# Four GpSimd operations of a recurrent layer moved to marked places in the step, and the product r put ahead of v

## The chip, the cores and the metric

The kernel runs on one core of one Trainium2 chip. The metric is the device time of one launch in microseconds: 3721.07 us, the median of 3 runs (3719.92 to 3722.31). Everything is float32.

A core has a TensorE for matrix products (PE in the profile; PEld are its weight loads), VectorE (DVE), ScalarE (ACT) and GpSimd (POOL) for elementwise work, and SyncE (SP), which issues most transfers. Each takes its own instructions in the order of the program and waits for the others by semaphores. GpSimd also issues some DMAs here, those that add into memory.

## What is computed

Four blocks follow each other on a tensor x of 4 batches x 512 tokens x 512 channels: a cross attention (layer 0), two recurrent layers of the RWKV kind (layers 1 and 2) and a resampler attention with an MLP (layer 3). The change touches only the recurrent layers. Both compute, for each batch, with `state` taken from the second input:

```python
xa = _ln(x, ln1_w, ln1_b)
sx = concatenate([state[:, 1][:, None], xa[:, :-1]], axis=1) - xa     # token differences
t = tanh((xa + sx * maa_x) @ maa_w1)                                  # then five mixes m
mw, mk, mv, mr, mg = ...                                              # t @ maa_w2, 5 x 512 channels
xw = xa + sx * (maa_w + mw)                                           # and xk, xv, xr, xg alike
w = exp(-exp(time_decay + tanh(xw @ decay_w1) @ decay_w2))
r, k, v = xr @ Wr.T, xk @ Wk.T, xv @ Wv.T
g = silu(xg @ Wg.T)
def step(s, (k, v, w, r)):                                            # per head, 16 x 16 state
    a = k[:, None] * v[None, :]
    return a + w[:, None] * s, einsum('s,st->t', r, u * a + s)
y = normalised(outs) * gn_w + gn_b                                    # per head
x = x + y * g @ Wo.T                                                  # time mixing
x = x + sigmoid(xr2 @ fWr.T) * (relu(xk2 @ fWk.T)**2 @ fWv.T)         # channel mixing, own norm and shift
```

The term `r * u * a` of the output needs no recurrence: it is v times the sum over a head's channels of r u k. The kernel calls that sum `al`.

## The kernel before

`recurrent` (from L455) works in 16 **units**: 2 layers x 4 batches x 2 halves of 256 tokens. A unit has 8 **steps**, one for each of 8 groups of state rows (two halves `e` of the value channels times four `i`). The main loop (L1078 and after) runs over a global step number g; step 0 to 7 of a unit in the text is g modulo 8. Two tokens are folded into one place of a scan, so that the scan has half as many places: the kernel keeps the tokens of a unit as firsts and seconds, and corrects for the fold with small products (`rk`, `D`, and the changed second half of r and first half of k).

One turn g of the loop issues, in this order:

- `summed(g - 1)` (L878): TensorE sums ry over state rows into PSUM tile py.
- `begun(g + 1)` (L825): VectorE makes kv and A, each a product of vr (v repeated over partitions, in PSUM) with o_k (L833), and copies the state into kv's column 0 (L839). GpSimd issues a DMA that adds A onto kv (`added`, L584). ScalarE copies the decays into W (L844). There are two kv buffers and one A.
- `scan(g)` (L860): VectorE's scan over kv with W (L866), then two products ry of kv with o_r (L871).
- every second half unit `repeated` (L808): TensorE makes vr from o_v.
- then what is due at this place of the step's four **phases** EARLY, SOON, MID, LATE. `mixes`, `outputs` and `channels` are generators; each `yield s, phase` says when its next part is issued, in steps from its unit's step 0. `mixes(q)` runs ahead of its unit (negative numbers), `outputs` and `channels` behind it. So in one turn of the loop three units are at work: with unit u in step 6, `mixes` prepares units u + 1 and u + 2, `outputs` finishes u - 1, `channels` u - 2.

The parts of `mixes(q)` that matter, with their places before: layer norm statistics (`stats`) at -11 LATE, `scaled` (z, ScalarE) at -10 EARLY, `turned` (transposes ptn on TensorE, emptied by ScalarE into xa) at -9 EARLY, `shift` (token differences sx, GpSimd, L588 and L589) at -9 MID, mixx at -9 LATE; the products k at -5 MID, v at -4 MID, r at -3 MID (for unit 0: r, then v), g at -2 MID, its gate (o_g, VectorE, L717) at -2 LATE. A product ends in ScalarE copies out of PSUM (L702); r's also makes `ruk`, r times u (L705). GpSimd multiplies ruk by k at -2 EARLY (L772). At step 0 TensorE forms al (L73), and at 0 LATE GpSimd makes y from v and al (L799) and adds rk to its second half (L800).

`outputs` normalises y: mean, squares, var, two powers on GpSimd (L933, L935), rp (ScalarE, L939), pbc (TensorE) and bc (ScalarE) at 13 EARLY, y times bc at 13 LATE (L946), then yg: scaled on ScalarE (L951), times g on GpSimd (L958), at 14 EARLY, and the product with Wo at 15 MID, added to x by VectorE (L973). `channels` has its own statistics, scaling, transposes (xc), shift (sxc) and products fk, fr, fv.

TensorE's products all use the line of the helper `mm` (L73), except those with 32 columns (L689 for v and g, L814 vr, L885 py). They share three PSUM buffers. Weights are loaded ahead into four SBUF buffers from SyncE's queue, in the order in which the products stand.

## Time and profile before

| What | us |
|---|---|
| median of 3 runs | 3721.07 (3719.92 to 3722.31) |
| span of the profiled execution, first to last instruction | 3715.9 |
| first scan to last scan of the recurrent layers, from the span's start | 780.6 to 2241.9 |
| busy in the span: TensorE, VectorE, ScalarE, GpSimd | 3545.8, 2728.7, 1675.7, 1743.4 |

The profiled execution's own time is its span; what lies outside the span (the launch's beginning and end) is in the runs' times only. A row of the timeline view reads: start, duration, engine, line, operation, what it writes <- what it reads, sizes (out<-in), how many equal ones are merged, and in brackets how long the engine was idle before it and what ended that. A row of the groups view reads: line, engine, operation, names, sizes, count | busy us, mean ns of one | idle us before them and what ended it. A row of stretches gives from:to and length, then the busy us of PE, PEld, DVE, ACT and POOL with their instructions, the granted share of TensorE's clock, the DMA engines' busy share and GB/s.

### The profile page before, as it was taken

How to read it: one execution, taken by the hardware profiler on the slowest of the kernel's cores; microseconds unless marked ns; L12 is line 12 of the kernel's file. 1: busy time of each engine (PE TensorE's matmuls, PEld its weight loads, DVE VectorE, ACT ScalarE, POOL GpSimd, SP SyncE). 2: the span in 40 equal slices, each digit the busy share in tenths (PEclk: the TensorE clock that was granted, in tenths of full speed). 3: DMA queues.
4: the chain of work that ended last, by engine and by line, in shares of the span. 5: the costliest groups of instructions: out<-in, count | busy, mean ns of one | idle time of the engine just before them, and what ended most of it. 6: DMA issues, size and time to landing. Idle time of an engine off the chain costs nothing. (4 is left out here: it accounts for less than half of the span.)

```text
span 3715.9 us, 52436 instructions
## 1 busy us (share of the span) xinstructions
PE 3545.8 (95%) x20544; PEld 1885.9 (51%) x20544; DVE 2728.7 (73%) x4601; ACT 1675.7 (45%) x2550; POOL 1743.4 (47%) x850
## 2 busy tenths in 40 slices
PE   8999999998899999999999988999999999999989
PEld 3333333365566665666666644444455444544446
DVE  6777777679988888888888883388855676667531
ACT  4777676544444444444444433233344334434421
POOL 4777777524444444444444443065533343444430
PEclk9999999999999999999999998999999999999999
DMA  4000000056677777777777775300022212121223
GB/s 154 24 12 24 12 9 21 24 130 140 146 177 175 177 187 182 176 175 177 177 175 177 177 167 134 102 26 18 23 88 77 72 52 88 60 71 35 97 97 125
DMA packets 188806, 386.67 MB, mean 104 GB/s; under 512 B 18128, under 2 KB 44880, under 8 KB 186512
## 3 DMA queue, kind: packets, MB, share of 16 engines
q1 hardware_dynamic: 150256, 251.72, 21.2%
q0 software_dynamic: 38304, 131.61, 19.4%
q8 instruction: 162, 2.65, 0.3%
q14 instruction: 84, 0.69, 0.1%
HBM read 247.50 MB, written 4.19 MB: 68 GB/s over the span
## 5 line engine op out<-in xcount | busy, mean ns | idle before, releaser
L1253 POOL TENSOR_TENSOR acc<-acc,aT 128x2048 f32<-128x2048 f32 x96 | 436.2, 4544 | 336.2 <-ACT aT L1248 219.6
L292 POOL TENSOR_TENSOR aT<-aT,nmT 128x1536 f32<-128x1536 f32 x124 | 428.6, 3460 | 206.1 <-ACT aT L290 182.8
L254 DVE CUSTOM_DVE_ANT_0 sc<-psc,nm 128x512 f32<-128x512 f32 x512 | 353.8, 691 | 146.8 <-PE psc L242 89.1
L1237 DVE TENSOR_TENSOR aT<-pst,mb 128x512 f32<-128x512 f32 x512 | 317.5, 681 | 163.2 <-PE pst L1192 163.2
L871 DVE TENSOR_TENSOR ry<-kv,o_r 128x1024 f32<-128x1024 f32 x256 | 398.6, 1598 | 7.2 <-PE pm L73 0.5
L866 DVE TENSOR_TENSOR_SCAN kv<-W,kv 128x1032 f32<-128x1032 f32 x128 | 295.9, 2311 | 0.0
L584 POOL DMA_DIRECT2D kv<-A x127 | 111.4, 877 | 358.0 <-DVE kv L839 220.0
L290 ACT COPY aT<-pst 128x512 f32<-128x512 f32 x372 | 196.5, 594 | 177.2 <-PE pst L279 176.8
L298 ACT ACTIVATE aT<-aT 128x2048 f32<-128x2048 f32 x128 | 246.7, 1929 | 5.5 <-POOL aT L292 4.8
L73 PE MATMUL ph<-nT,l_m 128*128 128x256 f32 x1024 | 235.9, 385 | 0.0
L73 PE MATMUL po<-l_m,hT 128*128 128x512 f32 x512 | 233.1, 601 | 0.0
L73 PEld LDWEIGHTS ph<-nT,l_m 128*128 128x128 f32 x1024 | 191.8, 191 | 64.2 <-issue 24.8
L1206 DVE CUSTOM_DVE_ANT_0 sc<-psc,zeros,mx 128x512 f32<-128x512 f32 x256 | 176.6, 745 | 56.2 <-PE psc L1192 47.1
L279 PE MATMUL pst<-q,km 32*128 32x512 f32 x1024 | 206.3, 639 | 9.4 <-DVE mxs L254 5.8
L1248 ACT ACTIVATE aT<-aT 128x2048 f32<-128x2048 f32 x64 | 122.3, 1910 | 190.6 <-DVE aT L1237 185.7
L1246 ACT ACTIVATE aT<-aT,mc 128x2048 f32<-128x2048 f32 x64 | 128.1, 2002 | 162.6 <-DVE aT L1237 156.3
L1206 DVE CUSTOM_DVE_ANT_0 sc<-psc,nm 128x512 f32<-128x512 f32 x256 | 161.1, 684 | 52.2 <-PE psc L1192 52.2
L242 PE MATMUL psc<-km,q 32*128 32x512 f32 x1024 | 197.8, 650 | 0.8 <-ACT q L223 0.8
L885 PE MATMUL py<-ry,k 128*32 128x512 f32 x1024 | 161.9, 625 | 38.3 <-DVE ry L871 25.6
L1192 PE MATMUL pst<-q,kT 32*128 32x512 f32 x1024 | 183.1, 649 | 0.0
L1192 PE MATMUL psc<-kT,q 32*128 32x512 f32 x1024 | 171.0, 644 | 12.3 <-DVE aT L1237 11.5
L1251 POOL TENSOR_TENSOR acc<-aT 128x2048 f32<-128x2048 f32 x16 | 72.5, 4532 | 234.2 <-ACT aT L1246 234.2
(266 smaller groups left out, 6999.6 us busy)
## 6 DMA issues: line engine op xcount, KB each, us to landing
l_m<-in_L_W SPq DMA_DIRECT2D x64, 1024.0 KB, 5.1
kv<-A POOLq DMA_DIRECT2D x127, 516.0 KB, 6.1
L_wk<-in_L_Wk SPq DMA_DIRECT2D x16, 1024.0 KB, 8.0
L_wr<-in_L_Wr SPq DMA_DIRECT2D x16, 1024.0 KB, 7.2
L_wv<-in_L_Wv SPq DMA_DIRECT2D x16, 1024.0 KB, 5.8
L_wg<-in_L_Wg SPq DMA_DIRECT2D x16, 1024.0 KB, 7.6
L_wo<-in_L_Wo SPq DMA_DIRECT2D x64, 256.0 KB, 4.9
L_fk<-in_L_fWk SPq DMA_DIRECT2D x16, 1024.0 KB, 6.8
```

The lines of the kernel that those rows point to most:

```text
L73: nc.tensor.matmul(ps, lhsT, rhs, start=(i == 0), stop=(i == len(pairs) - 1))
L242: nc.tensor.matmul(psc, d["q"][g][rs, lt * P : (lt + 1) * P], d["km"][rs, a, :], start=True, stop=True, tile_position=(32 * r, 0),)
L254: nc.vector.tensor_tensor_reduce(sc, ps[r], d["nm"][lt], 1.0, -3.0e38, ALU.add, ALU.max, mxs[:, a, lt, c : c + 1])
L279: nc.tensor.matmul(pst, d["km"][rs, a, s * P : (s + 1) * P], d["q2", a][rs, :], start=True, stop=True, tile_position=(32 * r, 0),)
L292: nc.gpsimd.tensor_tensor(w[:, n:, :], w[:, n:, :], nmT[:, None, :].to_broadcast([P, NR - n, L]), ALU.add)
L298: nc.scalar.activation(w, w, AF.Exp)
L866: nc.vector.tensor_tensor_scan(flat(kv), flat(W[g % 2]), flat(kv), 0.0, ALU.mult, ALU.add)
L871: nc.vector.tensor_tensor(y, kv[:, 4 * h : 4 * h + 4, None, :TP].to_broadcast([P, 4, 2, TP]), d["r"][:, i].rearrange("p (o m) -> p o m", o ...
L1192: nc.tensor.matmul(psc, lhsT[rs], rhs[rs], start=True, stop=True, tile_position=(32 * r, 0))
L1206: nc.vector.tensor_tensor_reduce(sc, ps[r], d["nm"][a], 1.0, mx[:, 0, lt, r : r + 1] if a else 3.0e38, ALU.add, ALU.min, mx[:, a, lt, r : ...
L1237: nc.vector.tensor_tensor(w[:, r, :], ps[r], d["mb"][:, r, :], ALU.subtract)
L1253: nc.gpsimd.tensor_tensor(d["acc", m], d["acc", m], w, ALU.add)
```

## The change

Four operations on GpSimd are no longer issued where their generator stands, but put into a list for a global step (`pooled`, `slots`): sx at step -9, ruk times k at -2, y at 1, its second sum at 2. `begun(g + 1)`, in turn g, issues that turn's list: after VectorE's kv and A products it first lets GpSimd copy one element per partition of kv into a new tile `mark`, which waits for kv's product, then issues the list, and only then the DMA that adds A onto kv. For units 0 and 1 the operations at negative steps are issued at once. The state's copy into kv's column 0 stands ahead of the kv and A products instead of behind them. r is made ahead of v in every unit. Statistics, scaling and transposes of `mixes` stand one step earlier from unit 2 on.

In the order of the instructions, in a unit of the middle: on TensorE r, py, pbc, v, py, vr, 16 transposes (xc and xa), g, py, Wo (before: v, py, pbc, r, py, vr, 8 transposes, g, py, 8 transposes, Wo). On ScalarE rp follows r's copies and the ruk scalings, the two z of the token mixing stand ahead of bc, and xa's copies ahead of yg. On VectorE the statistics stand in step 4 ahead of mix_g, and mixx ahead of the two additions to x. On GpSimd: mark, ruk, kv<-A, yg, sxc, mark, sx, kv<-A, xk, xr. Nothing else is added or removed but the marks.

```diff
@@ recurrent
+        mark = lp.tile([P, 1], F32, name="mark")
...
         st = {}
+        slots = {}
+
+        def pooled(q, at, f, *args):
+
+            if q < 2 and at < 0:
+                f(*args)
+            else:
+                slots.setdefault(G * q + at, []).append(lambda: f(*args))
@@ mixes
-            yield -12 if q == 1 else -10, EARLY
+            yield -12 if q == 1 else -11, EARLY
             z = scaled("mix", tiles, nm, rstd)
-            yield -11 if q == 1 else -9, EARLY
+            yield -11 if q == 1 else -10, EARLY
             turned(z, vec, cur, V_LN1W, V_LN1B)
...
-            yield -11 if q == 1 else -9, MID
+            yield -11 if q == 1 else -10, MID
...
-            shift(sx, cur, stT[:, :, b, 1] if hf == 0 else st[q - 1]["last"])
+            pooled(q, -9, shift, sx, cur, stT[:, :, b, 1] if hf == 0 else st[q - 1]["last"])
...
             yield -4, MID
-            if q > 0:
-                product("v")
-            else:
-                ruk = mp.tile(full, F32, tag="mix", name="ruk", bufs=BUFS["mix"])
-                product("r")
+            ruk = mp.tile(full, F32, tag="mix", name="ruk", bufs=BUFS["mix"])
+            product("r")
+            k, r = d["k"], d["r"]
+            pooled(q, -2, nc.gpsimd.tensor_tensor, ruk, ruk, k, ALU.mult)
             yield -4, LATE
             mixed("g")
             yield -3, MID
-            if q > 0:
-                ruk = mp.tile(full, F32, tag="mix", name="ruk", bufs=BUFS["mix"])
-                product("r")
-            else:
-                product("v")
+            product("v")
+            if q == 0:
                 repeated(0, 0)
             yield -2, EARLY
-            k, r = d["k"], d["r"]
-            nc.gpsimd.tensor_tensor(ruk, ruk, k, ALU.mult)
...
-            nc.gpsimd.tensor_tensor(y, d["v"], al[:, None, :].to_broadcast(full), ALU.mult)
-            nc.gpsimd.tensor_tensor(seconds(y), seconds(y), rk, ALU.add)
+            pooled(q, 1, nc.gpsimd.tensor_tensor, y, d["v"], al[:, None, :].to_broadcast(full), ALU.mult)
+            pooled(q, 2, nc.gpsimd.tensor_tensor, seconds(y), seconds(y), rk, ALU.add)
@@ begun
+            nc.vector.tensor_copy(quarters(kv)[:, :, :, 0], states(q)[:, i, e])
             for half, dst in ((seconds, kv), (firsts, A)):
                 nc.vector.tensor_tensor(
...
-            nc.vector.tensor_copy(quarters(kv)[:, :, :, 0], states(q)[:, i, e])
+            large = slots.pop(g - 1, ())
+            if large:
+                nc.gpsimd.tensor_copy(mark, kv[:, 0, 1:2])
+            for f in large:
+                f()
@@ the loop's start
-                follow(q, (-13 if q == 1 else -11, LATE), mixes(q))
+                follow(q, (-13 if q == 1 else -12, LATE), mixes(q))
```

## The prediction

> **What bounds the kernel now.** I read the page's busy shares first, then the recurrent stage (780 to 2250 us, the only one the diff touches) by stretches, then one unit of it in order of time, engine by engine.

> ```profile
> PE 3545.8 (95%) x20544; PEld 1885.9 (51%) x20544; DVE 2728.7 (73%) x4601; ACT 1675.7 (45%) x2550; POOL 1743.4 (47%) x850
> ...
> L871 DVE TENSOR_TENSOR ry<-kv,o_r 128x1024 f32<-128x1024 f32 x256 | 398.6, 1598 | 7.2 <-PE pm L73 0.5
> ```

> TensorE is the wall on average, but ry takes 1598 ns in the mean where its shortest is 1209 (view of tile ry): something lengthens it. By stretches (PE, PEld, DVE, ACT, POOL busy):

> ```profile
> 780.00:1037.00 257.00, 218.53 (x1738) 142.03 (x1737) 242.64 (x234) 109.08 (x223) 107.48 (x72) 0.93 0.64 143
> 1037.00:2090.00 1053.00, 1011.19 (x6890) 642.21 (x6889) 915.18 (x937) 490.35 (x1008) 483.31 (x341) 1.00 0.77 178
> ```

> Units 0 to 2 are bound by VectorE (242.6 of 257 us), units 3 to 13 by TensorE; scans eight steps apart show a unit to last 95.4 us there. The end of one such unit, TensorE:

> ```profile
> 1576.52 0.70 PE L73 MATMUL pbc<-rp,gsel 128*128 128x256 f32 x2 [0.74 <-ACT rp L939]
> 1577.06 7.63 PE L73 MATMUL pm<-mix_r,L_wr 128*128 128x256 f32 x32
> ...
> 1586.68 1.09 PE L572 MATMUL ptn<-ident,z 128*128 128x128 f32 x8
> 1587.71 7.14 PE L689 MATMUL pm<-mix_g,L_wg 128*32 128x256 f32 x128
> 1594.66 1.04 PE L885 MATMUL py<-ry,k 128*32 128x512 f32 x8
> ...
> 1596.89 0.66 PE L572 MATMUL ptn<-ident,z 128*128 128x128 f32 x4 [0.59 <-DVE o_g L717]
> 1597.53 7.11 PE L73 MATMUL pm<-L_wo,yg 128*128 128x512 f32 x16
> 1605.43 2.19 PE L885 MATMUL py<-ry,k 128*32 128x512 f32 x8 [0.80 <-DVE ry L871]
> ```

> The last row matters: py waits 0.80 us for the first ry, and takes 2.19 instead of 1.04 because the second ry is late as well. So one chain per unit ends last: g product, its gate o_g (ScalarE, then VectorE), step 7's kv, A, scan and two ry, then py and al. VectorE and GpSimd there:

> ```profile
> 1597.35 1.22 DVE L833 TENSOR_TENSOR kv<-vr,o_k 128x1024 f32<-128x1024 f32 x1
> 1598.48 1.21 DVE L833 TENSOR_TENSOR A<-vr,o_k 128x1024 f32<-128x1024 f32 x1
> ...
> 1599.68 2.30 DVE L866 TENSOR_TENSOR_SCAN kv<-W,kv 128x1032 f32<-128x1032 f32 x1
> 1602.02 4.50 DVE L871 TENSOR_TENSOR ry<-kv,o_r 128x1024 f32<-128x1024 f32 x2
> ```

> ```profile
> 1595.44 1.89 POOL L588 TENSOR_TENSOR sxc<-xc 128x1020 f32<-128x1020 f32 x1
> ...
> 1602.07 2.22 POOL L588 TENSOR_TENSOR sx<-xa 128x1020 f32<-128x1020 f32 x1
> 1603.92 1.51 POOL L589 TENSOR_TENSOR sx<-stT,xa 128x4 f32<-128x4 f32 x1
> ```

> The two ry take 4.50 beside sx and 2.36 where GpSimd is quiet (at 1574.56): 2.14 us lost. ruk does the same in step 6 (4.54 at 1585.13), y in step 0 (4.32 at 1518.46). sxc, beside o_g and kv, which read PSUM, lengthens nothing. The question is what the marked place does to the **scan**, which reads W and kv, both in SBUF. One place answers:

> ```profile
> 2241.88 3.98 DVE L866 TENSOR_TENSOR_SCAN kv<-W,kv 128x1032 f32<-128x1032 f32 x1
> ```

> ```profile
> 2240.84 2.86 POOL L588 TENSOR_TENSOR sxc<-xc 128x1020 f32<-128x1020 f32 x1
> ```

> A scan that comes up while sxc runs takes 3.98 instead of 2.30 and ends 2.2 us after sxc does: it waited for it. (At 1517.08 y starts inside a scan and takes 3.49: there GpSimd waited.) So whoever comes second waits, scans included.

> **The change, part by part.** Zero is 1567.83, where TensorE starts the first of the two products v and r in that unit; g ends at 26.83 (1594.66).

> 1. *r ahead of v.* pbc waits for rp, which ScalarE copies behind the product's own eviction. Behind v that is one o_v copy, and pbc starts 1.78 after py (1574.74 to 1576.52). Behind r the row at 1584.72 (o_r, 0.59) is followed by the ruk scalings (to 1586.05) and only then by rp (1.00): 2.43 after py. **+0.65.** vr then follows v with one py between: o_v's last copy ends 0.84 after that py starts, vr is due 0.99 after: nothing. The weight loads of r and v only change places on SP's queue, one product (7 us) apart.

> 2. *Layer norm, scaling and transposes a step earlier.* TensorE now turns four tiles (xc, xa) ahead of g instead of two: 2 x 0.515 (1586.68 to 1587.71) = **+1.03**. There are three PSUM buffers; ScalarE starts emptying 0.70 after the first tile and takes 0.97 a tile, so tile 4 waits 0.18 and g 0.45: **+0.63.** g ends 0.65 + 1.03 + 0.63 = 2.31 later, at 29.14. The 0.59 wait of the second ptn behind o_g goes, but that was beside the chain, not in it.

> 3. *From g to step 7.* Now kv starts 2.69 after g's end (1594.66 to 1597.35), because the o_g row on ScalarE (1595.51) waits for yg on GpSimd to free the buffer. After, yg's scaling follows xa instead of z (2.07 instead of 1.43 behind xc), yg ends at about 28.9, just before g; o_g then costs its own copies and gate, 1.70. **-1.0.** Were yg 1 us later, this gain would be gone.

> 4. *sx at its mark in step 7.* kv 1.21, then the mark. No row has a 128x1 copy on GpSimd; the nearest small ones are 0.21 (L589 beside sxc) and 0.84 (L552, blocked), so with its wait 0.15 to 0.9, and I take 0.3, near the first. sx by start-to-start spacing is 1.85 (1602.07 to 1603.92). It ends 3.4 after kv's start; the scan, due at 2.3, waits 1.1. Then scan 2.30, 0.1 for L589, two ry 2.36, and 0.07 for the moved state copy: 8.2 instead of 9.17. **-0.95.** The mark delays what is queued behind it on GpSimd: kv<-A by some 3.5 us (its second half waits for the scan), xk and xr by some 2.5. kv<-A was issued at 1600.32, lands in 4.6 in this step, and the next A comes at 1610.35: 5.4 of slack. xk lands some 6 us ahead of its product. Both covers hold.

> Sum for units 3 to 13: 0.65 + 1.03 + 0.63 - 1.0 - 0.95 = +0.36, 11 units: **+4**. TensorE would be ready for py 1.8 us ahead of ry, so the chain decides. y (step 1), its sum (step 2) and ruk (step 6) save or cost VectorE 0.4 to 2 us each, but VectorE then waits anyway (4.07 for o_g, 3.70 for S, 1.33 for mean): nothing. kv<-A behind y keeps 2.7 to 3.5 us of slack in step 1, less the 2.1 that y adds.

> [...] GpSimd's rows overlap (sx 2.22 from 1602.07, L589 from 1603.92). [...] By the printed 2.22 the unit would come to 0.37 more, 4 us in all; the duration 1.89 of the undisturbed sxc speaks for the spacing.

> 5. *Units 0 to 2.* Where VectorE decides, each move gains ry's loss and pays the scan's: y 2.0 against 1.35, ruk 2.0 against 1.35, sx 1.5 against 1.15, and the sum in step 2 newly costs 0.45 of a scan. Against it, the layer norm's 1.9 us of VectorE now stands ahead of step 5's A, and the next A waits for the DMA of that one (1.67, 1.60, 1.71 us in these units), so it moves 1.9. In unit 0 the gate also comes later, with g behind the transposes: the A at 840.89 becomes about 842.5, and o_g 854 instead of 851.1. By unit +2.5, 0, +0.5: **+3**. Bounds -8 (every contention gone) and +8.

> 6. *Units 14 and 15.* rp's 0.65 once; in unit 15 ry gains 2, which A gives back waiting for its DMA (it waited 0.97 already), and the sum costs 0.45: **+1.**

> Total 4 + 3 + 1 = +8 to +9. The profiled span of 3715.9 us becomes about 3724.5; the median shown, 3721.07, lies 5.2 above the span, and I carry that: **3730 us.**

> **Rivals.**
> *A, the forecast (0.58).* The mark moves the collision from ry to the scan, and g comes later. Own range 3718 to 3744: per unit -0.3 to +1.2 (mark 0.15 to 0.9, yg in time or not).
> *B, faster (0.21).* GpSimd's operations fit beside A, and the scan doesn't wait. Step 7 then takes 7.0, TensorE decides, and al starts at 38.4 instead of 39.7: -1.3 x 11 = -14, and units 0 to 2 gain 8: 3700 us (3692 to 3712). For it: 51 of 52 scans beside GpSimd are not lengthened. Against it: in those GpSimd had come second. It decides if sx ends within about 2.3 us of kv's start.
> *C, nothing (0.12).* Each move trades like for like, TensorE's order absorbs the rest: 3721.
> *D, clearly slower (0.09).* GpSimd reaches the mark late. It must finish sxc 1.0 us ahead of kv's end; if ScalarE's longer way to yg eats that, sx falls behind the scan and ry pays 2.1 as before, while g is still 2.3 later: +1.3 to +2.3 a unit, +8 for the rest: 3746 (3739 to 3752).

> **How the numbers follow.** A measurement of this kernel tells about 0.2% (7.4 us) from no change. A's range lies above 3728.5 in two thirds of its cases and within in the rest: slower 0.39 + 0.09 = 0.48, same 0.19 + 0.12 = 0.31, faster 0.21. The range 3704 to 3748 leaves out half of B and of D, some 0.16.

> **What would show it.** Right: ry near 1230 ns throughout and scans in steps 1, 6 and 7 at 3.3 to 3.8; pbc waiting about 1.4; two ptn rows in front of g with a wait ahead of it; py in step 7 still waiting for ry, by more than 0.8. Wrong: scans at 2.30 with ry at 1.2 (B), or ry still at 3.3 in step 7 (D), or a unit shorter than 95 us.

## The result, and the profile after

The changed kernel takes 3775.61 us, the median of 4 runs (3774.95 to 3777.61), against 3720.57 (3719.92 to 3722.31) before: 1.0148 times as long, 95% interval 1.0133 to 1.0162. That is 55 us more, where the prediction had 9 and a range that ended at 3748.

The span of the profiled execution grew by 60.0 us, 3715.9 to 3775.9. Scans eight steps apart tell where:

| Stretch of the profiled span | before | after | more | forecast |
|---|---|---|---|---|
| start to first scan | 780.6 | 783.2 | 2.6 | 0 |
| units 0 to 2 | 256.9 | 269.4 | 12.4 (unit 0 alone: 10.3) | 3 |
| unit 3 | 97.1 | 97.8 | 0.8 | 0.4 |
| units 4 to 13 | 955.6 | 989.6 | 34.0 | 3.6 |
| start of unit 14 to last scan | 151.7 | 155.9 | 4.2 | 1 |
| behind the last scan | 1474.1 | 1480.0 | 6.0 | 0 |

The page of the changed kernel has these lines (engine and line, names, sizes, count, then busy us and mean ns, then idle us ahead of them and what ended it):

```profile
PE 3572.3 (95%) x20544; PEld 1898.9 (50%) x20544; DVE 2674.5 (71%) x4601; ACT 1676.0 (44%) x2550; POOL 1751.0 (46%) x910
...
L874 DVE TENSOR_TENSOR_SCAN kv<-W,kv 128x1032 f32<-128x1032 f32 x128 | 337.2, 2634 | 0.2 <-DMA kv<-A 0.2
L879 DVE TENSOR_TENSOR ry<-kv,o_r 128x1024 f32<-128x1024 f32 x256 | 303.8, 1228 | 6.8
...
L837 DVE TENSOR_TENSOR A<-vr,o_k 128x1024 f32<-128x1024 f32 x128 | 155.7, 1217 | 59.0 <-DMA kv<-A 58.9
```

VectorE is busy 54 us less: ry fell from 1598 to 1228 ns, and the scan rose from 2311 to 2634. So the collision did move from ry to the scan, and in VectorE's busy time the move paid. But A, a single buffer, waited 59 us in all for the transfer that adds it onto kv, against 17.5 before:

```profile
L833 DVE TENSOR_TENSOR A<-vr,o_k 128x1024 f32<-128x1024 f32 x128 | 155.3, 1213 | 17.5 <-DMA kv<-A 17.4
```

Half of the 59 fall into units 3 to 13, where none of TensorE's waits ends with them; of the rest, 8.35 us in unit 0 cost time, as a run below shows.

The stretches, units 0 to 2 and units 3 to 13 (columns as in the prediction):

```profile
783.00:1052.00 269.00, 227.12 (x1736) 145.46 (x1735) 229.03 (x234) 108.31 (x223) 106.13 (x83) 0.88 0.60 134
1052.00:2147.00 1095.00, 1028.93 (x6913) 650.13 (x6912) 884.13 (x944) 492.48 (x1011) 493.01 (x386) 0.99 0.74 173
```

VectorE, which bound units 0 to 2 with 242.6 of 257 us, now waits there: 229.0 of 269. TensorE in a unit of the middle; the places that the prediction spoke of:

```profile
1611.22 0.70 PE L73 MATMUL pbc<-rp,gsel 128*128 128x256 f32 x2 [1.29 <-ACT rp L947]
...
1622.61 0.66 PE L573 MATMUL ptn<-ident,z 128*128 128x128 f32 x4 [0.24 <-ACT xc L575]
1623.52 7.14 PE L698 MATMUL pm<-mix_g,L_wg 128*32 128x256 f32 x128 [0.25 <-ACT xc L575]
...
1639.04 2.19 PE L893 MATMUL py<-ry,k 128*32 128x512 f32 x8 [0.46 <-DVE ry L879]
1641.16 1.99 PE L73 MATMUL al<-ruk,ksel 128*128 128x256 f32 x8
...
1649.59 7.14 PE L73 MATMUL pm<-xk,L_fk 128*128 128x256 f32 x32 [1.97 <-issue]
```

Up to al all is nearly as forecast. Then the product fk waits 1.97 us, where in the kernel before it had waited for nothing:

```profile
1612.09 1.91 PE L633 MATMUL pm<-mixx,L_w 128*32 128x256 f32 x8
1613.94 7.17 PE L73 MATMUL pm<-xk,L_fk 128*128 128x256 f32 x32
```

The view names only "issue", but xk's transfer landed at 1649.50, 0.09 us ahead of this row, and that distance is 0.09 us in each of units 3 to 13. GpSimd there:

```profile
1633.54 0.19 POOL L845 COPY mark<-kv 128x1 f32<-128x1 f32 x1 [1.21 <-DVE kv L837]
1633.68 1.89 POOL L589 TENSOR_TENSOR sx<-xa 128x1020 f32<-128x1020 f32 x1
1635.53 2.21 POOL L590 TENSOR_TENSOR sx<-stT,xa 128x4 f32<-128x4 f32 x1
1637.67 0.88 POOL L585 DMA_DIRECT2D kv<-A  x1
1638.26 1.18 POOL L585 DMA_DIRECT2D xk<-xc  x1
```

ScalarE had xk ready at 1634.1; it waited behind the mark, sx, the small second part of sx (2.21 us: it came up during the scan, which ended at 1637.73, and ended at 1637.74) and kv<-A. And the transfer itself was slower. The view of tile xk, units 3 to 13, before and then after:

```profile
DMA to landing us min/median/max: 6.3/6.4/6.6
```

```profile
DMA to landing us min/median/max: 11.0/11.2/11.5
```

The weights L_wk, 1 MB from SyncE's queue, start when Wo ends (0.03 us behind it, before and after). Before, that was 3.15 us behind xk's issue; after, 0.4 us (xk's issue and L_wk's before, then L_wk's after, beside the xk row above):

```profile
1601.51 0.86 POOL L584 DMA_DIRECT2D xk<-xc  x1 [0.31 <-ACT xk L996]
1604.66 0.37 SPq L63 DMA_DIRECT2D L_wk<-in_L_Wk  x1
```

```profile
1638.62 0.37 SPq L63 DMA_DIRECT2D L_wk<-in_L_Wk  x1
```

L_wk became slower as well: in units 3 to 13 it lands 9.4 to 10.4 us after its issue, where it took 7.9 to 8.2.

A unit grows for one more reason, the granted clock (share of TensorE's clock is the third figure from the end):

```profile
1662.89:1666.30 3.41, 2.91 (x17) 1.92 (x18) 3.00 (x3) 2.65 (x7) 0.01 (x1) 1.00 0.47 165
1666.30:1669.71 3.41, 3.41 (x5) 1.35 (x4) 3.41 (x5) 0.85 (x3) 3.14 (x5) 0.50 0.64 121
1669.71:1673.13 3.42, 3.42 (x9) 1.52 (x8) 3.39 (x3) 0.08 (x1) 0.85 (x1) 1.00 1.06 199
```

For 3.41 us TensorE ran at half its clock (0.50), at a cost of half of that, 1.7 us. In units 3 to 13 this happens twice in the kernel before and six times after. For a unit of 4 to 13, then: al 0.54 us later (50.83 against 50.29 from the start of k), fk another 2.04, and 0.8 for the clock: 3.4, ten times 34.

### The profile page after: what moved, and what is told of

It reads as the page before. It is cut to its first block, busy times and chain, and to the rows that moved or that the text cites. A ratio compares the mean times of both kernels' runs of the same rounds, so it can differ in the third digit from the quotient of the medians.

```text
span 3775.9 us, 52473 instructions
## 1 busy us (share of the span) xinstructions
PE 3572.3 (95%) x20544; PEld 1898.9 (50%) x20544; DVE 2674.5 (71%) x4601; ACT 1676.0 (44%) x2550; POOL 1751.0 (46%) x910
## 4 chain that ended last, share of the span: by engine, by line
PE 78%; DVE 9%; ACT 5%; issue 3%; DMA 2%; POOL 2%; SPq 0%; DVEq 0%; POOLq 0%; ACTq 0%
PE pm L73 12%; PE pv L73 6%; PE ph L73 6%; PE po L73 6%; PE psc L242 5%; PE pst L279 5%; PE pst L1200 4%; PE psc L1200 4%; PE pm L698 3%; PE po L304 3%; PE pr L73 3%; PE po L1266 3%; PE pk L73 3%; PE pmm L663 2%; DVE kv L874 2%
## 5 line engine op out<-in xcount | busy, mean ns | idle before, releaser
L874 DVE TENSOR_TENSOR_SCAN kv<-W,kv 128x1032 f32<-128x1032 f32 x128 | 337.2, 2634 | 0.2 <-DMA kv<-A 0.2
L879 DVE TENSOR_TENSOR ry<-kv,o_r 128x1024 f32<-128x1024 f32 x256 | 303.8, 1228 | 6.8
L73 PE MATMUL ph<-nT,l_m 128*128 128x256 f32 x1024 | 237.0, 387 | 0.0
L73 PE MATMUL po<-l_m,hT 128*128 128x512 f32 x512 | 233.1, 602 | 0.0
L73 PEld LDWEIGHTS ph<-nT,l_m 128*128 128x128 f32 x1024 | 192.9, 192 | 64.1 <-issue 24.8
L837 DVE TENSOR_TENSOR A<-vr,o_k 128x1024 f32<-128x1024 f32 x128 | 155.7, 1217 | 59.0 <-DMA kv<-A 58.9
```

Of the source, the lines that this page charges most:

```text
L73: nc.tensor.matmul(ps, lhsT, rhs, start=(i == 0), stop=(i == len(pairs) - 1))
L874: nc.vector.tensor_tensor_scan(flat(kv), flat(W[g % 2]), flat(kv), 0.0, ALU.mult, ALU.add)
L879: nc.vector.tensor_tensor(y, kv[:, 4 * h : 4 * h + 4, None, :TP].to_broadcast([P, 4, 2, TP]), d["r"][:, i].rearrange("p (o m) -> p o m", o ...
```

## Experiments

Theory 1 (late transfers): the marks and ruk hold DMAs back on GpSimd's queue until they run beside a weight load and beside each other, and land after they are due. Theory 2 (TensorE's order): r ahead of v and the earlier transposes make the loss. Each time below is a median, with the ratio to the kernel before on the same chip.

**sx taken out of the list** (against the changed kernel).

```diff
-            yield -11 if q == 1 else -10, MID
+            yield -11 if q == 1 else -9, MID
...
-            pooled(q, -9, shift, sx, cur, ...)
+            shift(sx, cur, ...)
```

> The changed kernel with sx alone taken out of the list: it stands at -9 MID again, behind kv<-A and xk on GpSimd's queue. Theory 1 (late transfers): in the changed kernel the mark, sx and its small second part hold kv<-A and xk back by 3 to 4 us, so that xk's transfer falls together with those of kv<-A, xr and the weights L_wk and takes 11.2 us instead of 6.3; fk then waits some 2.0 us a unit, and behind that idle stretch the granted clock drops in 7 of 11 units (about 1.7 us each). Taken out, xk lands in 6 to 7 us, fk waits for nothing, the clock stays; sx lengthens the two ry again (4.4 instead of 2.36), so a unit takes 96 to 97 us: 3743 to 3757 in all, forecast 3750. Theory 2 (TensorE's order): what makes fk late is r ahead of v and the four transposes ahead of g, which delay xc and with it xk; then fk waits as before, ry costs its 1 us more, and the time is 3775 to 3788.

Measured: 3760.95 us, 1.0105 (1.0088 to 1.0122). fk waits for nothing and units without a drop of the clock take 96.6 to 96.9, as theory 1 had it; xk lands in 7.5 to 7.7 us, a little above its 6 to 7. The time is 4 us above its range, because the clock, which was to stay, drops in 7 of 11 units: the drop does not need the wait at fk.

**The small part of a shift first** (against the changed kernel).

```diff
         def shift(sx, cur, before):
-            nc.gpsimd.tensor_tensor(sx[:, :, 1:], cur[:, :, : TS - 1], cur[:, :, 1:], ALU.subtract)
             nc.gpsimd.tensor_tensor(sx[:, :, 0], before, cur[:, :, 0], ALU.subtract)
+            nc.gpsimd.tensor_tensor(sx[:, :, 1:], cur[:, :, : TS - 1], cur[:, :, 1:], ALU.subtract)
```

> The changed kernel with the two parts of a shift exchanged: the small one (128x4) ahead of the large one. In the changed kernel the small part comes up while the scan runs, waits for all of it (2.21 us) and holds kv<-A and xk back with it. Theory 1 (late transfers): kv<-A and xk are issued about 1.9 us earlier, fk's wait falls from 2.0 us to between 0 and 0.8, the clock drops seldom; the scan waits 0.1 to 0.2 longer. Units of 96.0 to 97.2 us: 3741 to 3756, forecast 3748. Theory 2 (TensorE's order): nothing but the 0.2 us a unit: 3773 to 3779.

Measured: 3743.17 us, 1.0061 (1.0046 to 1.0076), 32 us less for two exchanged lines. GpSimd, and below it the view of tile xk:

```profile
1620.12 0.19 POOL L845 COPY mark<-kv 128x1 f32<-128x1 f32 x1 [1.22 <-DVE kv L837]
1620.26 0.21 POOL L589 TENSOR_TENSOR sx<-stT,xa 128x4 f32<-128x4 f32 x1
1620.42 1.89 POOL L590 TENSOR_TENSOR sx<-xa 128x1020 f32<-128x1020 f32 x1
1622.25 0.88 POOL L585 DMA_DIRECT2D kv<-A  x1
1622.84 1.18 POOL L585 DMA_DIRECT2D xk<-xc  x1
```

```profile
DMA to landing us min/median/max: 7.1/7.6/8.1
```

xk is issued 2.7 us behind the mark instead of 4.7, 2.4 us ahead of L_wk instead of 0.4, and lands 3.3 to 4.4 us before fk begins. Units 3 to 13 take 96.1 us, and 97.7 where the clock drops, which it does in four of them. Theory 2 is out as the cause of fk's wait.

**A quarter of L_wk** (against the changed kernel). The product k uses the first quarter of its weights four times, so that much of the weights is left out.

```diff
+        if name[-2:] == "wk":
+            nc.sync.dma_start(w[:, 0], src[:P])
+            return w
...
-    mm(pm[:, a, :], [(perm(wx[:, k], i + a), ms[x][:, k, :]) for k in range(KC)])
+    mm(pm[:, a, :], [(perm(wx[:, k if x == "r" else 0], i + a), ms[x][:, k, :]) for k in range(KC)])
```

> The changed kernel, but of each L_wk only the first quarter is transferred (256 of 1024 KB), and the product k uses that quarter in place of all four: a part of the weights is left out, the instructions of all engines are the same. It tells what lengthens xk's transfer. Theory 1: the weights L_wk, which start 0.4 us behind xk instead of 3.15; with a quarter of them xk lands in 7 to 9 us instead of 11.2, fk waits for nothing, and the time falls by 20 to 33 us, to 3742 to 3756. Rival: the two neighbours on GpSimd's own queue, kv<-A 0.6 us ahead and xr 0.5 to 1.6 behind; then xk keeps 10 us or more, fk waits 1 us or more, and the time is 3762 or more.

Measured: 3737.48 us, 1.0047 (1.0032 to 1.0062). xk stays behind mark, sx and kv<-A as in the changed kernel, with the same neighbours on GpSimd's queue, and yet:

```profile
DMA to landing us min/median/max: 7.7/7.8/7.8
```

So it is the weight load beside it that makes 11.2 us of 7.8. fk waits for nothing, and a unit takes 95.9 us. The time is 4.5 us below the expected range: unit 1 gained too (81.8 us instead of 86.6, where A waits 0.75 us instead of 4.60), which was not in the forecast.

**r u k of unit 1 in the list** (against the changed kernel).

```diff
-            if q < 2 and at < 0:
+            if q == 0 and at < 0 or q == 1 and at < -2:
```

> The changed kernel, with r u k of unit 1 put into the list as in all later units, instead of being issued at once. Theory 1: issued at once, it stands ahead of the power of the norm and of the DMA of mix_g on GpSimd, so that mix_g and kv<-A are issued 0.6 us apart beside the weights L_wv, kv<-A takes 10.7 us instead of 8.7 at a later issue, and A waits 8.35 us. In the list, mix_g goes out some 5 us ahead of kv<-A and unit 0 takes 86 to 89 us instead of 94.4: 3767 to 3771. Rival: the wait of A in unit 0 comes from the norm's statistics and the product r, which stay where they are; then it keeps most of its 8 us: 3774 to 3777.

Measured: 3760.64 us, 1.0108 (1.0092 to 1.0123), 15 us less; unit 0 takes 84.6 us instead of 94.4, more than I expected. These 10 us are the edit's; in the profiled spans the rest of the gain lies in unit 14 (3.0) and behind the last scan (3.7), and its cause is not shown. GpSimd and VectorE in unit 0 of the changed kernel:

```profile
834.87 2.40 POOL L598 TENSOR_TENSOR ruk<-ruk,o_k 128x1024 f32<-128x1024 f32 x1 [7.63 <-ACT ruk L714]
...
840.70 0.91 POOL L585 DMA_DIRECT2D mix_g<-xa  x1
841.31 1.18 POOL L585 DMA_DIRECT2D kv<-A  x1
```

```profile
852.07 1.22 DVE L837 TENSOR_TENSOR A<-vr,o_k 128x1024 f32<-128x1024 f32 x1 [8.35 <-DMA kv<-A]
```

GpSimd stands 7.63 us at ruk, which needs the product r, and mix_g and the norm's power stand behind it. So mix_g, kv<-A and the weights L_wv (issued at 841.37) start within 0.7 us, and kv<-A lands after 10.7. With ruk out of the way, mix_g is issued at 834.41, kv<-A at 836.08, L_wv at 840.41; kv<-A takes 7.0, and A waits:

```profile
843.11 1.22 DVE L837 TENSOR_TENSOR A<-vr,o_k 128x1024 f32<-128x1024 f32 x1 [1.57 <-DMA kv<-A]
```

**Both mends** (the two edits above, against the changed kernel).

> The changed kernel with both mends: the small part of a shift ahead of the large one, and r u k of unit 1 in the list. If the late transfers are two separate losses, their gains add up: 3743.2 - 15 = 3728 (3724 to 3734), with unit 0 at 84 to 87 us and no wait ahead of fk. If they are one loss seen twice, about 3740.

Measured: 3731.82 us, 1.0032 (1.0019 to 1.0045). The gains add to within 4 us: mending two late issues on GpSimd's queue gives back 44 of the 55 us. That includes what went with them: in units 4 to 13 the clock drops 3 times instead of 6, some 5 us, and in the profiles 4 us lie behind the last scan, which neither edit touches.

**r ahead of v alone** (against the kernel before; the exchange of the two products as in the change, ruk where it was).

```diff
-            if q > 0:
-                product("v")
-            else:
-                ruk = ...
-                product("r")
+            ruk = ...
+            product("r")
```

> The kernel before with r ahead of v in every unit and nothing else. Theory 1: pbc waits about 1.3 to 1.4 us instead of 0.74 (rp stands behind the scalings of r), units of 95.4 to 96.1 us, xk lands as before: 3720 to 3731, forecast 3728. Theory 2 (TensorE's order): more than 1 us a unit and a wait ahead of fk: 3735 or more.

Measured: 3745.28 us, 1.0068 (1.0053 to 1.0083): theory 1's forecast of 3728 missed, and the time is one that theory 2 had, though fk waits for nothing. al comes 1.0 us later and not 0.65: pbc waits 1.29 us instead of 0.74, and r, no longer behind that wait, takes 7.84 us instead of 7.63; some 0.2 is spread over smaller gaps. That is 10 us in units 4 to 13. The new length of a unit, 96.4 us, then meets a drop of the clock in five units of eleven: another 6.5 us. The rest lies mostly in units 0 to 2 (4.3 us in the profiles) and behind the last scan (5.2), and its cause is not shown.

**Norm and transposes earlier alone** (against the kernel before).

```diff
-            yield -12 if q == 1 else -10, EARLY
+            yield -12 if q == 1 else -11, EARLY
...
-            yield -11 if q == 1 else -9, EARLY
+            yield -11 if q == 1 else -10, EARLY
```

> The kernel before with the statistics, scaling and transposes of the token mixing one step earlier and nothing else (sx stays at -9 MID, r behind v). By the prediction's terms g ends 1.03 + 0.63 us later and step 7 begins 1.0 earlier behind it, so al moves by +0.7 us a unit: 3726 to 3736, forecast 3730, the more if the new length of the unit meets more drops of the granted clock. Theory 2 (TensorE's order makes the loss of the whole change): 3745 or more.

Measured: 3734.49 us, 1.0049 (1.0032 to 1.0066), on the upper side. Where nothing else is late a unit takes 95.6 us, 0.2 more than before. But the statistics hold a kv<-A back until L_fk's load begins (issued 0.25 us apart, kv<-A took 11.9 us), A waits up to 3.7 us and vr behind it up to 2.3, and units of 96.8 to 99.3 stand between the short ones, the longest with a drop of the clock as well. The same loss again, at another transfer.

**r u k, y and its sum listed alone** (against the kernel before: `pooled`, `slots` and the mark, with three of the four operations).

> The kernel before with r u k, y and its second sum put into the list (marks in steps 6, 1 and 2 of a unit), and nothing else: r behind v, norm and sx as before. The prediction held these for nothing in units 3 to 13 and a few us in units 0 to 2. Theory 1: their marks delay kv<-A in those steps by 2 to 4 us, but TensorE does not wait for it: 3716 to 3726. Rival: kv<-A comes so late that A, a single buffer, waits in steps 1, 2 and 7 and the unit grows by 0.5 us or more: 3728 to 3745.

Measured: 3719.01 us, 0.9995 (0.9986 to 1.0004): nothing, as the prediction had it.

Alone, then, r ahead of v costs 24 us, the earlier norm 14 and the three operations nothing, while the whole change with both mends costs 11. What an edit costs by itself is not its share of the 55 us: each alone meets drops of the clock and late transfers of its own. sx listed alone was not tried.

**sx behind ry** (against the kernel before): the mark copies an element of the step's second ry, and stands where sx stood.

```diff
+            if ys:
+                nc.gpsimd.tensor_copy(mark, ys[max(ys)][:, 3, 1, TP - 1 :])
             shift(sx, cur, stT[:, :, b, 1] if hf == 0 else st[q - 1]["last"])
```

> The kernel before with one instruction more a unit: a mark on GpSimd ahead of sx at -9 MID, which copies one element of the step's second ry and so waits for it; sx then runs beside the additions to x, which read PSUM. If the lock on the two ry is what ends step 7 (they take 4.5 us there instead of 2.36, py waits 0.8 us and takes 2.19 instead of 1.04), py follows Wo at once in 1.04 us, al starts 1.5 to 1.9 us earlier and a unit takes 93.5 to 94 us: 3692 to 3706, forecast 3698. Rival: sx and xr, issued 2.5 us later, make mixx or pr late instead; then the unit stays at 95 us or grows: 3715 or more.

Measured: 3710.93 us, 0.9973 (0.9963 to 0.9983). What the two ry lose beside sx was worth what the kernel before suggested: TensorE goes from Wo to py to al without a wait, and a unit takes 93.5 us, 1.9 less:

```profile
1592.19 7.11 PE L73 MATMUL pm<-L_wo,yg 128*128 128x512 f32 x16
1599.22 1.06 PE L888 MATMUL py<-ry,k 128*32 128x512 f32 x8
1600.22 1.99 PE L73 MATMUL al<-ruk,ksel 128*128 128x256 f32 x8
```

But eight of eleven units meet a drop of the clock and take 95.1, so that half of the gain was given back, and the time missed its range.

**sx and y behind ry**: the same mark ahead of y as well.

> The kernel with sx behind ry (n1_sx_behind_ry), and y in step 0 put behind the step's second ry by a mark as well. In units 3 to 13 VectorE waits in the steps after anyway, so nothing; in units 0 to 2, which VectorE binds, the two ry of step 0 fall from 4.3 us to 2.36: 2 us a unit, 4 to 6 in all. Against 3710.9 of n1_sx_behind_ry: 3703 to 3708. Rival: y then ends later and holds kv<-A of the next step or the sum of y back: no gain, 3710 to 3714.

Measured: 3706.16 us, 0.9959 (0.9945 to 0.9974), within the expected range. The intervals of this run and the last overlap, so the gain of 5 us is not clear of noise; in the profiles units 0 to 2 take 252.9 us instead of 255.8, 3 us less where 4 to 6 had been expected.

**Narrow products in halves** (against sx behind ry).

```diff
-            second("wk")
-            yield -7, MID if q == 1 else EARLY
-            second("vr")
+            second("wk", (0,))                # q == 1: as before
+            yield -7, EARLY
+            second("wk", (2,))
+            yield -7, MID
+            second("vr", (0,))
             yield -7, LATE
             mixed("wk")
+            yield -6, EARLY
+            second("vr", (2,))
```

> The kernel with sx behind ry, and the two stretches of narrow products (pmm, 32 rows of 128, 3.2 us with their gap) broken from unit 2 on: half of the first behind pmean, the first half of the second behind pr, its other half behind vr. In the traces so far every drop of the granted clock in units 3 to 13 lasts 3.41 us, starts on a grid of 3.41 us and follows a grid window that one of these stretches fills. Theory: with no such stretch there is no such drop; n1_sx_behind_ry has 8 of them (1.7 us each), so 10 to 14 us go: 3697 to 3702, units of 93.3 to 94 us without exception. Rival: the drops follow TensorE's idle time, whatever the products, or the halves bring waits of their own for mix_w and mix_v: 3706 to 3718.

Measured: 3733.32 us, 1.0032 (1.0021 to 1.0044): slower than either theory allowed. The drops behind the narrow products are gone, and others have come behind idle time: the second product of the decays (td @ decay_w2, just ahead of product k) waits nine times in units 3 to 13, 23.9 us in all, for VectorE to empty pv, and drops follow, six of 6.8 to 10.2 us and two of 3.4. VectorE is late: y makes the two ry of step 0 take 4.33 instead of 2.36, and kv<-A beside L_wr takes 9.7 us, for which A waits (1150 to 2080 us):

```profile
L847 DVE TENSOR_TENSOR A<-vr,o_k 128x1024 f32<-128x1024 f32 x77 | 93.5, 1214 | 35.7 <-DMA kv<-A 35.7
```

**Both: y behind ry too, and the narrow products in halves.**

> Both together: sx and y behind ry, and the narrow products in halves. If each works and they are independent, the gains add up: 3692 to 3699. If one of them does not work, the time is that of the other alone.

Measured: 3673.59 us, 0.987 (0.9853 to 0.9886), 48 us faster than the kernel before and better than both expectations. A waits 6.4 us in that stretch instead of 35.7, so y was what had made VectorE late. The halves stand apart, and the two waits between them (0.59 and 0.50 us a unit) went: the two stretches took 3.21 and 3.11 us, the four halves take about 1.07 each:

```profile
1694.46 1.99 PE L73 MATMUL pmean<-y,gmean 128*128 128x256 f32 x8
1696.38 1.13 PE L658 MATMUL pmm<-th,L_w 32*128 32x256 f32 x8
1697.45 7.13 PE L73 MATMUL pr<-L_fr,xr 128*128 128x512 f32 x16
1704.51 1.13 PE L658 MATMUL pmm<-th,L_w 32*128 32x256 f32 x8
```

Units 3 to 13 take 91.6 to 91.7 us, all but one, which idles 3.0 us and then has half the clock for 10.2.

## Why the prediction was wrong

*What bounds the kernel:* right. What sx adds to the two ry at the end of step 7 (4.50 us instead of 2.36) was worth 1.9 us a unit, as the run with sx behind ry shows.

*Step 1, r ahead of v,* was mis-sized: pbc's wait grew by 0.55 (forecast 0.65), but r by itself also takes 0.25 more when it no longer follows that wait, and alone the edit cost 1.0 a unit (there r takes 0.21 more). "vr after v costs nothing" held.

*Step 2, transposes:* the waits were 0.24 and 0.25 (forecast 0.18 and 0.45); g ended 29.43 us after the first of the two products, forecast 29.14. *Step 3:* kv's products came 1.79 behind g's end, forecast 1.70; yg was in time.

*Step 4, sx at its mark,* first half right: mark 0.19, spacing 1.85, scan 3.20 us (0.9 of waiting, forecast 1.1), ry 2.36. From the first product to al it is 40.11 us against 39.72: +0.39, where the sum had +0.36. That closeness is partly luck: kv's products in step 7 started 0.38 later than forecast, and from there to the end of ry it took 7.85 us instead of 8.2. py's wait for ry, which was to exceed 0.8, is 0.46.

*The step that failed is the end of step 4, "Both covers hold."* It moved xk's issue by 2.5 us against 6 us of cover, at the transfer time of before. The issue moved about as foreseen (3.1 us against al), but the transfer time was no constant: moved into the start of L_wk's load, it went from 6.4 to 11.2 us, and 3.1 + 4.8 us used up the cover. I had priced the place in GpSimd's queue, and not what else the DMA engines carry at the new time. The run with a quarter of L_wk has both sides: with the issue still late, but the load small, fk does not wait, and the unit is 0.5 us longer than before, near the forecast's 0.36.

*The same error in step 5.* For units 0 to 2 the sum had +3 with bounds of 8; unit 0 alone lost 10.3. The delay of the DMAs behind a moved operation was counted for sx and y, but not for ruk of unit 1, which the list exempts: issued with r, it stood ahead of mix_g for 7.63 us. y's slack in step 1 did hold: the kv<-A behind y (issued at 1656.34) landed at 1664.25, and the next A came at 1667.92. But A waited 2.31 in step 1 itself (at 1654.57) for the kv<-A of step 0, which no mark delays: it took 9.0 us, with L_wk, xk and xr still on their way when it was issued. *Step 6* has +4.2 instead of +1; with both mends the stretch from unit 14 to the last scan takes 149.6 us, 2.1 less than before.

*Not in the prediction at all:* the granted clock, some 8 us in units 4 to 13.

*Rivals.* A was the right case with the wrong size. D, slower by 25 through GpSimd being late at the mark, had GpSimd's lateness on the wrong side: it reached the mark in time, and its queue was late behind it. With both mends the kernel takes 3731.8, 2 us from the forecast of 3730. Part of that is luck: units 4 to 13 still take 10 us more than before, where the sum had 3.6, and units 3 and 14 less.

Open: the 2.6 us ahead of the first scan, of which r ahead of v alone brings 0.9, and the 6.0 behind the last one. The latter stretch takes 1473.3 to 1480.0 us in the fourteen traces, 1480.0 also with a quarter of L_wk and 1474.1 with the small part first, so its cause is not shown.

## What to carry to other kernels

When an edit delays the issue of a DMA, its cover is not the old slack less the delay: look up what other queues start at the new time, because they can lengthen the transfer: here xk, issued 0.4 us ahead of a 1 MB weight load, took 11.2 us, where it had taken 6.4 issued 3.15 us ahead, and 7.8 beside a quarter of that load. An operation that can block (a mark: 1.21 us here, a product not yet made: 7.63, a small operation that comes up during a scan: 2.21) belongs behind the DMAs that others wait for, and a collision is better removed by moving one operator past the work that it disturbs (sx behind ry: 1.9 us a unit less) than by letting it fall on an earlier instruction of the same chain (sx at its mark: the scan 3.20 instead of 2.30). After any change of the length of a loop, read the granted clock before the sum is judged (two units of eleven with a drop at 95.4 us a unit, eight at 93.5).

## What the runs showed of the hardware

```profile
1645.83:1649.24 3.41, 1.79 (x8) 0.68 (x7) 3.38 (x3) 0.74 (x2) 0.57 (x1) 1.00 1.09 230
1649.24:1652.65 3.41, 3.06 (x14) 2.76 (x15) 3.02 (x5) 0.00 (x0) 0.33 (x2) 1.00 1.06 211
```

  Idle windows are followed by drops as well: one that was busy 1.39 us precedes the drop of 10.2 us in the last run, and one of 1.12 us the drop at 1205.75 with the norm earlier, which is the exception to "every drop" in what was expected of the halves. Apart from these two and the eight of the run with halves alone, the fourteen traces have 55 drops in units 3 to 13, and each follows a window that falls onto a stretch of pmm. In those 55 windows all other products were busy at most 0.60 us; in the 375 windows with over 1 us of pmm that no drop followed, at least 0.61. (Before and after alone: 0.37 to 0.56 us in the eight windows ahead of a drop, 0.67 or more in 77 without.) So what told them apart in these traces is how little a window held beside narrow products. A unit of 95.4 us is 27.95 windows, and the place shifts little from unit to unit: two drops. At 96.4 us (28.24) or 93.5 (27.39) it wanders, and five units of eleven are hit with r ahead of v alone, eight with sx behind ry. That no drop followed a window with halves of 1.13 us, in two runs of eleven such units, supports that; whether it is the 32 rows that matter was not tried by itself.
- *A scan that waits.* In steps 1, 6 and 7 of the unit shown the scan took 2.30, 3.71 and 3.20 us; in steps 6 and 7 VectorE comes second to GpSimd's ruk and sx and waits, as the one row of before had suggested. In step 1, forecast like them, A's wait had let y end first; with the small part first, where A hardly waits there, that scan takes 3.4 to 3.7 us in nine of eleven units. The small part of sx, which comes up during the scan of step 7, took 2.21 us and held up the queue behind it; with the small part first it took 0.21.
